# Layer 0's k and v from 15 block products each in place of 18, q plain; the third pair's table products within k's set; the feed-forward's last additions on GpSimd

## The chip, the cores and the metric

The kernel runs on one core of a Trainium2 chip. The metric is the device time of one execution in microseconds (us). A core has TensorE (PE; PEld is its loading of the stationary operand), VectorE (DVE), ScalarE (ACT), GpSimd (POOL) and SyncE (SP). ScalarE, VectorE and GpSimd work through queues in the order that is written for them; GpSimd and SyncE also issue most DMA transfers. Results of TensorE go to PSUM, eight banks of 128 x 512 numbers; everything else on the chip is in SBUF.

## What is computed

Two layers on eight images of 32 x 32 positions and 384 channels. Layer 0 is attention over all 1024 positions of an image, six heads of 64, with a table term that depends on the distance of rows and of columns; layer 1 is causal attention with one head of 384 and a feed-forward with binarized weights. Cut to what matters:

```python
qkv = x.reshape(b, hw, c) @ qkv_w + qkv_b           # x: group-normed image
attn = einsum('bqd,bkd->bqk', q * SCALE, k) + rel_h + rel_w
x = x + softmax(attn) @ v @ proj_w + proj_b         # layer 0
t = t + causal_attention(layer_norm(t))             # layer 1
h = gelu(quantize(layer_norm(t) @ sign(W1 - mean) + b1))
t = t + quantize(h @ sign(W2 - mean) + b2)
# quantize(y) = clip(y * 128 / (max|y| + eps), -128 + eps, 128 - eps); the feed-forward is zero for images 5 to 7
```

## The kernel before, in words

Images are taken in the order 5, 0, 1, 2, 3, 4, 6, 7 (`ORDER`). The feed-forward runs for 0 to 4; its ending for one image (`finish`, from the list `unfinished`) is issued within layer 0 of the next. Everything is float32, and the whole program is written out without loops on the chip. A scheduler orders each engine's queue as the program is built, by the order of the Python lines as far as data, buffers and explicit `issue_after` edges let it.

An image is held transposed, `xT` (`gnT`): channels on 128 partitions in three blocks, 1024 positions in the free dimension.

*Layer 0, products.* `project_qk` (L438) makes one third m of q or k: for each half of 512 positions three products of a 128 x 128 block of `wqkv_sb` (stationary) with 512 positions, added in one PSUM bank. m = 0 to 2 are q, 3 to 5 are k. `queries_keys` copies the two banks out, one on ScalarE (L468) and one on VectorE (L466); k is written with a stride of two. For images that follow a feed-forward, the products of m = 0 and 1 are made within it (`ahead`). `positions(p)` (L484) multiplies q of a pair p of heads with the table `rel`; ScalarE (L489) and VectorE (L490) copy the results out, and SP transfers turn them into `near` by way of DRAM (L496, L501). `values(j)` (L536) makes v for 128 positions: three products with positions as the stationary operand and 384 columns of weights. So k and v are 3 x 2 x 3 = 18 blocks of 128 x 128 by 512 each. `place(p)` rounds `near` to a high part (ScalarE, L517) and a remainder (VectorE, L519) and issues 16 transfers (L524), eight on SP and eight on POOL, into four image buffers `r`.

*Layer 0, attention.* For each pair and half, eight scores (L588, k with q, then L592, `r` with the fixed matrix `unit`), Exp on ScalarE (L598), sums on VectorE (L605), products with v (L613). Then the projection (L386).

*Layer 1* (L734, L386, L775, L790), during which the next image's group norm runs; then the feed-forward: first product L898, Gelu L924 and L925, second product L939, VectorE adds the bias (L940) and takes the maximum; GpSimd reduces it over partitions (L854), clips (L949), VectorE multiplies and adds to x (L953), and four output transfers are issued on POOL (L994).

*Buffers.* `image` is a pool of 11 buffers of 128 x 3080 numbers (images, q, k, v, r, x, weights of the feed-forward), `page` one of 12 buffers of 128 x 1024; every PSUM tile is one of the eight banks.

## Time and profile before

| what | us |
|---|---|
| median of 3 runs (2350.43 to 2351.89) | 2351.74 |
| the profiled execution, its own time | 2350.82 |
| its span, first to last instruction | 2348.8 |
| L438, 576 records, busy | 257.4 |
| L536, 384 records, busy | 125.2 |
| L484, 192 records, busy | 47.7 |
| L953, VectorE, 40 records, busy | 26.1 |
| L949, GpSimd, 40 records, busy | 30.5 |

A line of the profile's fifth part names the line of the kernel, engine and operation, result<-operands, shapes and count, then busy time and mean length of one, then the idle time of the engine just before and what ended it. Rows of time show start and length. Successive records of TensorE overlap, since the ends are modelled, so the distance of two starts tells what one costs. One float32 product stands as two load records and two matmul records.

### The profile page before, as it was taken

Reading aid. Unit: us, or ns where it says so; the run is one execution under the profiler, and the core shown is the slowest. Engines: PE = TensorE matmul, PEld = TensorE weight load, DVE = VectorE, ACT = ScalarE, POOL = GpSimd, SP = SyncE. Lnnn points to the kernel's source line nnn. Section 1 sums busy time; section 2 is a strip of 40 time slices with the busy share of each in tenths; the row PEclk is TensorE's granted clock in tenths of the full one; section 3 lists DMA queues with packets and bytes.
Section 4 is the critical chain, followed back from the end, with each engine's and each line's share of the span. In section 5 each row is a group of like instructions: output and inputs, shape, how many; then the busy total and the mean of one; then the engine's idle time right before and its main releaser. Section 6 shows DMA issues by size and latency. Waiting matters only on the chain.

```text
span 2348.8 us, 26174 instructions
## 1 busy us (share of the span) xinstructions
PE 2324.9 (99%) x9442; PEld 1288.2 (55%) x9442; DVE 1433.9 (61%) x2302; ACT 1041.7 (44%) x1763; POOL 316.6 (13%) x421
## 2 busy tenths in 40 slices
PE   7999999999999999999999999999999999999998
PEld 3445544568545577445684455864457744554454
DVE  3685568665587347684466864558734668525851
ACT  3551156137463256642365522747324656115621
POOL 0420013000230001310002300023000131001300
PEclk9999999999999999999999999999999999999999
DMA  6431361130631003520107211063101262017100
GB/s 166 146 117 37 104 146 38 54 135 1 144 99 68 20 21 91 118 88 14 41 12 166 65 68 41 1 138 105 68 1 41 68 139 63 1 51 146 45 1 29
DMA packets 154795, 169.99 MB, mean 72 GB/s; under 512 B 113408, under 2 KB 126048, under 8 KB 153120
## 3 DMA queue, kind: packets, MB, share of 16 engines
q1 hardware_dynamic: 134416, 98.93, 17.2%
q0 software_dynamic: 17184, 69.22, 9.7%
q8 instruction: 77, 1.26, 0.2%
q10 hardware_dynamic: 3056, 0.08, 0.1%
q14 instruction: 62, 0.51, 0.1%
HBM read 75.38 MB, written 42.47 MB: 50 GB/s over the span
## 4 chain that ended last, share of the span: by engine, by line
PE 99%; DVE 1%; DMA 0%; issue 0%; ACT 0%; DVEq 0%
PE f_s L588 14%; PE f_av L613 14%; PE f_qk L438 11%; PE f_s L775 8%; PE f_av L790 8%; PE f_y L939 7%; PE f_y L898 7%; PE f_pj L386 5%; PE f_v L386 5%; PE f_v L536 5%; PE f_q L734 5%; PE f_s L592 4%; PE f_rel L484 2%; PE f_pt L314 1%; PE f_den L631 0%; DMA f_gnT<-in_xT 0%
## 5 line engine op out<-in xcount | busy, mean ns | idle before, releaser
L598 ACT ACTIVATE f_pr<-f_s 128x512 f32<-128x512 f32 x768 | 413.6, 595 | 54.2 <-PE f_s L592 46.8
L588 PE MATMUL f_s<-f_q,f_k 64*128 64x512 f32 x1536 | 399.0, 595 | 0.0
L605 DVE TENSOR_TENSOR f_sum<-f_sum,f_pr 128x1024 f32<-128x1024 f32 x288 | 365.8, 1270 | 22.6 <-ACT f_pr L598 0.5
L613 PE MATMUL f_av<-f_pr,f_v 128*64 128x512 f32 x1536 | 339.4, 594 | 0.0
L592 PE MATMUL f_s<-f_r,unit 64*128 64x512 f32 x768 | 307.6, 792 | 0.0
L438 PE MATMUL f_qk<-f_gnT,wqkv_sb 128*128 128x512 f32 x576 | 257.4, 600 | 1.5 <-DVE f_gnT L349 1.5
L588 PEld LDWEIGHTS f_s<-f_q,f_k 64*128 64x128 f32 x1536 | 145.7, 186 | 127.4 <-issue 67.3
L613 PEld LDWEIGHTS f_av<-f_pr,f_v 128*64 128x64 f32 x1536 | 106.2, 137 | 196.3 <-issue 192.4
L775 PE MATMUL f_s<-f_q,f_lnT 128*128 128x512 f32 (+3 forms) x576 | 195.9, 488 | 0.0
L790 PE MATMUL f_av<-f_v,f_pr 128*128 128x385 f32 x576 | 195.3, 486 | 0.0
L438 PEld LDWEIGHTS f_qk<-f_gnT,wqkv_sb 128*128 128x128 f32 x576 | 108.0, 191 | 143.2 <-issue 131.5
L784 ACT ACTIVATE f_pr<-f_s 128x512 f32<-128x512 f32 (+3 forms) x96 | 47.1, 491 | 267.7 <-DVE f_s L780 220.7
L524 POOL DMA_DIRECT2D f_r<-f_far x192 | 102.2, 535 | 461.7 <-DVE f_far L519 450.9
L790 PEld LDWEIGHTS f_av<-f_v,f_pr 128*128 128x128 f32 x576 | 108.2, 190 | 77.3 <-issue 11.5
L775 PEld LDWEIGHTS f_s<-f_q,f_lnT 128*128 128x128 f32 x576 | 102.0, 190 | 77.8 <-issue 53.8
L902 ACT ACTIVATE f_h<-f_y,b_sb 128x256 f32<-128x256 f32 x240 | 100.9, 472 | 67.5 <-PE f_y L898 66.9
L909 DVE TENSOR_REDUCE am<-f_h 128x1 f32<-128x1024 f32 (+2 forms) x80 | 71.5, 946 | 96.3 <-ACT f_h L902 96.3
L734 PE MATMUL f_q<-f_lnT,wqk 128*128 128x512 f32 x288 | 127.5, 592 | 0.0
L386 PE MATMUL f_pj<-wproj_sb,f_oT 128*128 128x384 f32 x384 | 127.3, 488 | 0.0
L386 PE MATMUL f_v<-wv_sb,f_lnT 128*128 128x384 f32 x384 | 126.5, 486 | 0.0
L536 PE MATMUL f_v<-wqkv_sb,f_gnT 128*128 128x384 f32 x384 | 125.2, 486 | 0.0
L592 PEld LDWEIGHTS f_s<-f_r,unit 64*128 64x128 f32 x768 | 75.1, 187 | 90.0 <-issue 90.0
(153 smaller groups left out, 3024.9 us busy)
## 6 DMA issues: line engine op xcount, KB each, us to landing
f_far<-f_far SPq DMA_DIRECT2D x48, 512.0 KB, 3.2
f_r<-f_far POOLq DMA_DIRECT2D x192, 128.0 KB, 3.9
f_r<-f_far SPq DMA_DIRECT2D x192, 128.0 KB, 3.2
f_gnT<-in_xT SPq DMA_DIRECT2D x24, 512.0 KB, 4.6
f_x<-in_x SPq DMA_DIRECT2D x32, 384.0 KB, 7.5
out_y<-f_x POOLq DMA_DIRECT2D x28, 384.0 KB, 4.4
f_far<-f_far SPq DMA_DIRECT2D x128, 64.0 KB, 4.9
f_w1a<-w1s POOLq DMA_DIRECT2D x5, 1536.0 KB, 7.0
```

What stands on the lines that cost most here:

```text
L386: nc.tensor.matmul(ps[:, :C], xT[:, k, ts(j, P)], w[:, k, cols], start=(k == 0), stop=(k == NC - 1))
L438: nc.tensor.matmul(made[half], wqkv_sb[:, i, ts(m, P)], xT[:, i, ts(half, 512)], start=(i == 0), stop=(i == NC - 1))
L536: nc.tensor.matmul(ps, keys[:, i, j // 2, j % 2], wqkv_sb[:, i, 2 * C :], start=(i == 0), stop=(i == NC - 1))
L588: nc.tensor.matmul(sc[par], k[rows[par], p, ts(c, P)], q[rows[par], p, ts(half, 512)], start=True, stop=False)
L592: last_matmul[0] = nc.tensor.matmul(sc[par], unit[rows[par], c // 2 % 2].rearrange("i h w -> i (h w)"), r[2 * (c // 4) + c % 2][rows[par], ...
L598: last_exp[0] = nc.scalar.activation(pr[:, ts(par, 512)], sc[par], AF.Exp).ins
L605: adds.append(nc.vector.tensor_tensor(total, total, pr, ALU.add).ins)
L613: last_matmul[0] = nc.tensor.matmul(av[ts(par, HD), :], v[:, c, ts(2 * p + par, HD)], pr[:, ts(par, 512)], start=(c == 0), stop=(c == NJ - 1),
L734: nc.tensor.matmul(ps, wqk[:, k, ts(m, P)], xT[:, half, k, :], start=(k == 0), stop=(k == NC - 1))
L775: nc.tensor.matmul(sc[:, lo:], xT[:, c // 4, k, ts(c % 4, P)], q[:, half, k, lo:], start=(k == 0), stop=(k == NC - 1),)
L790: nc.tensor.matmul(av[:, : C + 1], prs[c][:, ts(j - c, P)], v[:, c, :], start=(c == 0), stop=(c == j))
L898: nc.tensor.matmul(ps, w1k[i // 2][:, ts(m, P)], xs[i % 2][:, half, i // 2, :], start=(i == 0), stop=(i == 2 * NC - 1))
```

## The change

k and v are each made by a scheme that multiplies a 3 x 3 block matrix (weights) with a 3 x 2 one (three channel blocks by two halves of positions) in 15 block products. Each product takes a sum of weight blocks (`weight_forms`, 15 forms for k and 15 for v, made once on GpSimd into `wf`) and a sum of image blocks (`image_forms`, ten made and five given; the same forms serve k and v; on VectorE for the first image, on GpSimd during layer 1 for the others). `ProductSet` runs the products in the order `PROD_ORDER` into six banks A to F. After ten of the products the running content of the bank is copied out on ScalarE (`keep`), while the bank goes on being added to; four pairs of such copies are subtracted on VectorE, and six final VectorE additions of a bank and a kept part write k or v. For v each product is four pieces with 128 positions as the stationary operand and 128 columns of weights. q stays as it was, from its own `wq_sb`.

All of these matmuls, q's and the tables' are chained in their written order (`in_turn`). The third pair's table products stand after k's fifth product; after the eighth and the eleventh, ScalarE's two rounding copies of the first pair's `near` are put between the bank copies; the load of the Exp table follows k's last bank copy. The first pair's remainders follow k's last addition.

In the feed-forward x is written to DRAM (`spilt`) and read back later, the activations lie in image buffers rather than pages, and the ending (scale and clip, second clip, addition to x) runs on GpSimd alone. The image pool has 10 buffers, the first pair's `near` lies in an image buffer, `r` takes three buffers rather than four. A second path for out-of-range sums, not taken with these inputs, stays plain.

```diff
...
+N_PROD = 15
+PROD_ORDER = (
+    ("A", 5, "m5"), ("B", 11, "m11"), ("C", 7, "m7"), ("A", 13, "n0"), ("B", 6, "n1"), ("D", 8, None),
+    ("A", 12, "n2"), ("B", 0, "n4"), ("E", 14, None), ("A", 4, "n3"), ("B", 1, "n5"), ("F", 9, None),
+    ("A", 10, "n6"), ("B", 3, None), ("A", 2, None),
+)
+PROD_ENDS = {
+    "D": ("n2", "n2", 0, 0, 1), "E": ("m7", "n3", 0, 1, 1), "F": ("n0", "n1", 1, 0, 1),
+    "B": ("m5", "m5", 1, 1, -1), "A": ("n4", "n4", 2, 0, -1), "C": ("n5", "n6", 2, 1, 1),
+}
+PROD_TILES = (0, 2, 1)
+PROD_COMBINE = {"n1": ("n0", "n1"), "n2": ("n2", "m11"), "n3": ("m7", "n3"), "n6": ("n5", "n6")}
+PROD_PAGES = (("m11", "n1"), ("m5", "n4"), ("n2", "m7"), ("n0", "n3"), ("n5", "n6"))
+X_MADE = (2, 5, 0, 1, 11, 4, 7, 13, 6, 12)
+X_GIVEN = {8: (0, 0), 14: (0, 1), 9: (1, 0), 3: (1, 1), 10: (2, 1)}
...
-        self.image_ = pool("image", 11)
+        self.image_ = pool("image", 10)
...
+    wf, wq_sb = tile_of("wf", [P, N_PROD, 2, P]), tile_of("wq_sb", [P, NC, C])
...
+        raw = [wq_sb]
         for i in range(3):
-            nc.sync.dma_start(out=wqkv_sb[:, :, ts(i, C)], in_=src[:, :, ts(i, C)])
+            if i:
+                raw.append(pools.flat(f"raw_{i}")[:, : NC * C].rearrange("p (k o) -> p k o", k=NC))
+            nc.sync.dma_start(out=raw[i], in_=src[:, :, ts(i, C)])
...
+        nc.scalar.mul(bqk_neg, bqk, -1.0)
...
+    def weight_forms(pools, eng, raw, s):
...
+        room = pools.page(f"wsum_{s}")
+        s1, s2 = room[:, :P], room[:, P : 2 * P]
...
+        def w(i, k):
+            return raw[:, k, ts(PROD_TILES[i], P)]
+        def f(r):
+            return wf[:, r, s - 1, :]
...
+        add(s1, w(0, 1), w(0, 2))
+        add(f(8), w(0, 0), s1)
+        add(s2, w(2, 0), w(2, 2))
+        add(f(9), w(2, 1), s2)
+        sub(f(14), w(0, 0), w(0, 1))
+        sub(f(14), f(14), w(1, 0))
+        add(f(5), w(0, 1), w(2, 0))
+        eng.tensor_scalar_mul(f(11), w(0, 1), -1.0)
+        eng.tensor_copy(f(13), w(2, 0))
+        add(f(6), f(5), w(2, 2))
+        add(f(12), s1, w(2, 0))
+        add(f(0), w(1, 1), s2)
+        add(f(4), s1, w(1, 0))
+        eng.tensor_copy(f(1), w(1, 1))
+        add(f(10), f(12), w(2, 2))
+        sub(f(10), f(10), w(1, 2))
+        slowest = last[0]
+        eng.tensor_copy(f(7), w(1, 0))
+        sub(f(3), w(2, 1), w(2, 0))
+        sub(f(3), f(3), w(1, 1))
+        add(f(2), w(1, 0), w(1, 1))
+        add(f(2), f(2), w(1, 2))
+        return slowest
...
+        def in_turn(*args, **kw):
+            with tc.issue_after(last_product[0]) if last_product[0] else contextlib.nullcontext():
+                last_product[0] = nc.tensor.matmul(*args, **kw).ins
...
+        def image_forms(b, xT, eng):
+            rooms = [pools.page(f"xf_{b}_{i}") for i in range(len(X_MADE) // 2)]
+            made = {r: rooms[i // 2][:, ts(i % 2, 512)] for i, r in enumerate(X_MADE)}
+            def x(k, n):
+                return xT[:, k, ts(n, 512)]
+            def add(r, a, b, op=ALU.add):
+                eng.tensor_tensor(made[r], a, b, op)
+            def sub(r, a, b):
+                add(r, a, b, ALU.subtract)
+            f = made
+            sub(5, x(2, 1), x(0, 1))
+            sub(5, f[5], x(1, 1))
+            add(2, x(2, 0), x(2, 1))
+            sub(0, f[2], x(1, 0))
+            sub(1, x(1, 1), f[0])
+            add(11, f[1], x(0, 1))
+            sub(4, x(0, 0), f[2])
+            add(7, f[4], x(0, 1))
+            add(13, f[7], x(1, 1))
+            sub(6, x(1, 0), x(2, 0))
+            sub(12, x(2, 0), x(0, 0))
+            return made | {r: x(*at) for r, at in X_GIVEN.items()}
...
+        class ProductSet:
+            def __init__(self, b, s, forms):
+                self.name, self.s, self.forms = f"{b}_{s}", s, forms
+                self.at, self.banks, self.part, self.final = 0, {}, {}, None
+                self.left = {bank: sum(bank == o[0] for o in PROD_ORDER) for bank in "ABCDEF"}
+                self.full, self.behind = [], None
+            def kept(self, name):
+                if name not in self.part:
+                    pair = next(pair for pair in PROD_PAGES if name in pair)
+                    room = pools.page(f"u_{self.name}_{pair[0]}")
+                    self.part.update({n: room[:, ts(i, 512)] for i, n in enumerate(pair)})
+                return self.part[name]
+            def multiply(self, ps, r, start):
+                x, w = self.forms[r], wf[:, r, self.s - 1, :]
+                if self.s == 1:
+                    in_turn(ps, w, x, start=start, stop=True, skip_group_check=True)
+                    return
+                keys = x.rearrange("p (g i n) -> p g n i", g=2, n=2)
+                for j in range(4):
+                    in_turn(
+                        ps[:, ts(j, P)], keys[:, j // 2, j % 2], w, start=start and j == 0, stop=True, skip_group_check=True
+                    )
+            def keep(self, ps, name):
+                dst = self.kept(name)
+                end = next((end for end in PROD_ENDS.values() if end[0] == name), None)
+                with tc.issue_after(self.behind) if self.behind else contextlib.nullcontext():
+                    if self.s == 2 or end is None:
+                        self.last_copy = nc.scalar.copy(dst, ps).ins
+                        return
+                    m = NPAIR + end[2]
+                    bias = (bqk if end[4] > 0 else bqk_neg)[:, m : m + 1]
+                    self.last_copy = nc.scalar.activation(dst, ps, AF.Identity, bias=bias).ins
+            def run(self, n, final=None):
+                self.final = final or self.final
+                for self.now in range(self.at, self.at + n):
+                    bank, r, name = PROD_ORDER[self.now]
+                    start = bank not in self.banks
+                    if start:
+                        self.banks[bank] = pools.o_tile(f"pr_{self.name}_{bank}")
+                    self.left[bank] -= 1
+                    self.multiply(self.banks[bank], r, start)
+                    if name is not None:
+                        self.keep(self.banks[bank], name)
+                    if name in PROD_COMBINE:
+                        dst, other = PROD_COMBINE[name]
+                        nc.vector.tensor_tensor(self.part[dst], self.part[dst], self.part[other], ALU.subtract)
+                    if not self.left[bank]:
+                        self.full.append(bank)
+                    self.finish()
+                self.at += n
+            def finish(self):
+                while self.final and self.full:
+                    bank = next((f for f in self.full if self.ready(f)), None)
+                    if bank is None:
+                        return
+                    self.full.remove(bank)
+                    name, _, p, half, sign = PROD_ENDS[bank]
+                    self.last_final = self.final(self.banks.pop(bank), self.part[name], p, half, ALU.add if sign > 0 else ALU.subtract)
+            def ready(self, bank):
+                return PROD_ENDS[bank][1] in [o[2] for o in PROD_ORDER[: self.now + 1]]
...
-                    nc.tensor.matmul(
-                        made[half], wqkv_sb[:, i, ts(m, P)], xT[:, i, ts(half, 512)], start=(i == 0), stop=(i == NC - 1)
+                    (in_turn if pools.fast else nc.tensor.matmul)(
+                        made[half], w[:, i, ts(m, P)], xT[:, i, ts(half, 512)], start=(i == 0), stop=(i == NC - 1)
...
-            r = []
+            rooms = {}
+            def r(part, p):
...
+                i, at = divmod(4 * (p % 2) + part, NPAIR)
+                if i not in rooms:
+                    rooms[i] = pools.flat(f"r_{b}_{i}", F32R)
+                return rooms[i][:, ts(at, T)]
...
-                    if half:
+                    if half and not (pools.fast and b == ORDER[0]):
...
+            def round_off(d, near, pages):
+                hi, _, src = both(near, pages, d)
+                return nc.scalar.copy(hi, src).ins
...
+                    hi, lo, src = both(near, pages, d)
+                    if not rounded:
+                        with behind_of(behind[0]):
+                            round_off(d, near, pages)
+                    with behind_of(behind[1]):
                         nc.vector.tensor_tensor(lo, src, hi.bitcast(F32), ALU.subtract)
...
+            def put_keys(ps, kept, p, half, op):
+                dst = k[:, p, ts(half, 512)].rearrange("d (g n i) -> d g i n", n=2, i=P)
+                ps, kept = (t.rearrange("d (g i n) -> d g i n", n=2, i=P) for t in (ps, kept))
+                return nc.vector.tensor_tensor(dst, ps, kept, op).ins
+            def put_values(ps, kept, p, half, op):
+                ps, kept = (t.rearrange("t (j c) -> t j c", j=4) for t in (ps, kept))
+                return nc.vector.tensor_tensor(v[:, 4 * half : 4 * half + 4, ts(p, P)], ps, kept, op).ins
...
+            def products():
+                forms = xf.pop(b)
+                of_k, of_v = (ProductSet(b, s, forms) for s in (1, 2))
+                for m in range(NPAIR):
+                    queries_keys(m)
+                    if m:
+                        near.append(positions(m - 1))
+                of_k.run(5, put_keys)
+                near.append(positions(NPAIR - 1))
+                if unfinished:
                     unfinished.pop()()
-                    early = pools.small.tile([P, 1], F32, tag="early", name=f"early0_{b}")
-                    nc.scalar.activation(early, k[:, 0, T - 1 :], AF.Exp, scale=0.0)
-            for j in range(NJ):
-                values(j)
-            r.extend(pools.image(f"r_{b}_{part}", F32R) for part in range(4))
-            place(0, *near[0])
+                for d in range(2):
+                    of_k.run(3)
+                    with behind_of(of_k.last_copy):
+                        of_k.behind = round_off(d, *near[0])
+                of_k.run(N_PROD - of_k.at)
+                place(0, *near[0], (None, of_k.last_final), rounded=True)
+                early = pools.small.tile([P, 1], F32, tag="early", name=f"early0_{b}")
+                with behind_of(of_k.last_copy):
+                    of_v.behind = nc.scalar.activation(early, of_k.part["n5"][:, 0:1], AF.Exp, scale=0.0).ins
+                of_v.run(N_PROD, put_values)
...
+                            r(2 * (c // 4) + c % 2, p)[rows[par], ts(half, 512)], start=False, stop=True,
...
+            spilt = store.tile([P, NJ * C], F32, tag="spilt", bufs=2, name=f"{pools.path}_spilt_{b}")
...
+                    last_product[0] = last_transpose[0]
+                    ahead[AFTER[b], 0] = project_qk(AFTER[b], gn, 0, plain[0])
...
+            nc.sync.dma_start(out=spilt, in_=xt.rearrange("p j c -> p (j c)"))
...
+            def activate(room, j, m0, m1):
...
+                hi, lo = (room[:, i, m0:m1, :] for i in range(2))
...
+                room = pools.flat(f"hilo_{b}_{j}", F32R)[:, : 3 * T].rearrange("p (i m q) -> p i m q", i=2, q=P)
...
+                if j == 4:
+                    xt = pools.flat(f"xagain_{b}")[:, : NJ * C].rearrange("p (j c) -> p j c", j=NJ)
+                    nc.sync.dma_start(out=xt.rearrange("p j c -> p (j c)"), in_=spilt)
...
-            s, ga = absmax_scale(am2, f"2_{b}")
-            up = pools.small.tile([P, 1], F32, tag="qu", name=f"qu_{b}")
-            nc.vector.tensor_scalar_mul(up, ga, (QB - QEPS) / QB)
-            low = pools.small.tile([P, 1], F32, tag="ql", name=f"ql_{b}")
-            nc.vector.tensor_scalar_mul(low, up, -1.0)
+            s, _ = absmax_scale(am2, f"2_{b}")
             for j in range(NJ):
-                nc.gpsimd.tensor_scalar(y[:, j, :], y[:, j, :], up, low, ALU.min, ALU.max)
+                nc.gpsimd.tensor_scalar(y[:, j, :], y[:, j, :], s, QB - QEPS, ALU.mult, ALU.min)
             def add():
                 for j in range(NJ):
-                    nc.vector.scalar_tensor_tensor(xt[:, j, :], y[:, j, :], s, xt[:, j, :], ALU.mult, ALU.add)
+                    nc.gpsimd.tensor_scalar_max(y[:, j, :], y[:, j, :], QEPS - QB)
+                    nc.gpsimd.tensor_tensor(xt[:, j, :], y[:, j, :], xt[:, j, :], ALU.add)
+                return xt
...
+                xf[ORDER[0]] = image_forms(ORDER[0], gn, nc.vector)
+                with tc.issue_after(weight_forms(pools, nc.gpsimd, raw[1], 1)):
+                    weight_forms(pools, nc.gpsimd, raw[2], 2)
...
-                        yield from group_norm_T(AFTER[b])
+                        norm = group_norm_T(AFTER[b])
+                        made = next(norm)
+                        yield made
+                        next(norm, None)
+                        if pools.fast:
+                            xf[AFTER[b]] = image_forms(AFTER[b], made, nc.gpsimd)
...
```

## The prediction

> **What bounds the kernel now.** I read the busy times first, then the chain of waits, then TensorE's rows in order of time around one image's layer 0.
>
> ```profile
> PE 2324.9 (99%) x9442; PEld 1288.2 (55%) x9442; DVE 1433.9 (61%) x2302; ACT 1041.7 (44%) x1763; POOL 316.6 (13%) x421
> PEclk9999999999999999999999999999999999999999
> ...
> PE 99%; DVE 1%; DMA 0%; issue 0%; ACT 0%; DVEq 0%
> ```
>
> TensorE works or is modelled busy for 99% of the span at the full granted clock, and 99% of the chain that ended last is TensorE's own. Between 14.3 us and the closing test of the sums no row of it waits for more than 0.3 us. So a TensorE row that goes away shortens the kernel by its own spacing, as long as nothing new makes TensorE wait; and a wait that appears costs its full length.
>
> The rows of time (start, length, engine) of the image that begins at 595 us, one with a feed-forward ahead of it:
>
> ```profile
> 604.47 5.42 PE L438 MATMUL f_qk<-f_gnT,wqkv_sb 128*128 128x512 f32 x12
> 609.82 1.99 PE L484 MATMUL f_rel<-f_q,rel 64*128 64x512 f32 x8
> 611.74 10.57 PE L438 MATMUL f_qk<-f_gnT,wqkv_sb 128*128 128x512 f32 x24
> 622.14 15.64 PE L536 MATMUL f_v<-wqkv_sb,f_gnT 128*128 128x384 f32 x48
> 637.71 1.13 PE L588 MATMUL f_s<-f_q,f_k 64*128 64x512 f32 x4
> ```
>
> Lengths overlap at their ends, so I take differences of starts. k, the third table product and v last from 604.47 to 637.71, 33.24 us. Each product stands as two records. k: 5.35 + 10.40 = 15.75 us for 18 products, 0.858 us each (10.30 us for 12 in the chain of waits) and 0.3 us for changes between shapes. Table product: 1.92. v: 15.57 us for 24, 0.645 each. Image by image this stretch repeats eight times.
>
> **k.** 15 products of the same shape as L438: 15 x 0.858 + 0.3 = 13.17 us, 2.58 less per image.
>
> **v.** 15 products of four pieces, each 128 columns wide, two records each: 120 records. The nearest row is the last diagonal block of layer 1's scores, six records of that shape (start, length):
>
> ```profile
> 255.13 0.83 PE L775 MATMUL f_s<-f_q,f_lnT 128*128 128x128 f32 x6
> 255.80 2.44 PE L790 MATMUL f_av<-f_v,f_pr 128*128 128x385 f32 x7
> ```
>
> 0.67 us for six is 0.112 us a record, so 120 x 0.112 = 13.44 us. From below: if records went at the rate per column of L438 (0.429 us for 512 columns), 0.107, 12.87 us. From above: the stationary operand here is every second token, as in L536, whose load records take 196 ns where L775's take 190; if all 6 ns came on top, 0.118, 14.16 us. I take 0.115, 13.8 us: 1.77 less per image.
>
> The Trainium skill speaks against this part: "TensorE: Matmul & The Clock Gate", section "LDWEIGHTS (loading the stationary operand)", has a load cost its number of columns over 1.2 ns, so 107 ns however few columns follow it. By that estimate loads alone are 120 x 0.107 = 12.8 us, and the row, at 112 ns, agrees that a piece this narrow is no faster than its load.
>
> **What ScalarE now puts in TensorE's way.** A bank is copied out in the middle of its accumulation, and its next product must wait for that copy. I run the k set with t = 0 at its first product. Durations: a product 0.858; copy with bias 0.68 (L468, q), plain 0.59 (L660); from a product's end to ScalarE's start 0.31 (597.21 + 3 x 0.858 = 599.78, ScalarE starts at 600.09); back to TensorE 0.15 (L333 ends 10.74, TensorE starts 10.89). Now two rounding copies stand between the bank copies, by order:
>
> ```profile
> 616.85 1.07 ACT L517 CAST f_far<-f_near 64x1024 fp32r<-64x1024 f32 x1
> 624.78 1.99 ACT L517 CAST f_far<-f_near 64x1024 fp32r<-64x1024 f32 x1
> ```
>
> Five products to 4.29, the third table product to 6.21, D8, A12, B0 to 8.79. n4 is copied 9.10 to 9.78, first rounding to 10.85, n3 10.85 to 11.53, n5 (B1 ends 11.37) 11.68 to 12.36, second rounding to 14.35, n6 to 14.96. A10 ended at 13.08 and B3 at 13.94; A2, which adds into the bank that n6 is read from, starts at 15.11. That is a wait of 1.17 us in each image, and everything of TensorE's chained order is behind it. The earlier copies are done at least 0.4 us before they are needed: m5 is ready for A13 at 2.16 (ScalarE has the second table product's copies until 1.3), needed at 2.57. In the v set no rounding stands there; n6 is ready 0.31 + 0.59 + 0.15 = 1.05 after A10 while B3 covers 0.9: 0.15 us. The Exp table load (1.28) now falls between the sets, ahead of a copy needed only 1.8 us after its product.
>
> Stretch per image: 13.17 + 1.92 + 1.17 + 13.80 + 0.15 = 30.21 in place of 33.24: 3.03 saved, **24.2 us** for eight.
>
> **VectorE.** Per set four combinations (678 ns, VectorE's row of L657) and six final additions: k's write with the stride of L466 (1.12), v's near L666 (0.69). The k set, copies of the table product (2.8) and the rounding remainders (1.2 and 1.95) run to about t = 22 in my order, the v set's additions end about 1.8 after the last product; v is first read by L613, 8.9 us later. The banks: six of eight per set, the last three of k freed by t = 19, when v has three. Nothing on the path; without that cover a late k addition would delay the first scores one for one.
>
> **GpSimd.** The feed-forward's ending moves there on five images. VectorE loses 8 x 0.70 (L953), which were hidden. The rows of time (in brackets the idle time before and what ended it):
>
> ```profile
> 604.09 6.10 POOL L949 TENSOR_SCALAR f_y<-f_y,qu,ql 128x384 f32<-128x384 f32 x8 [6.90 <-PE f_rel L484]
> ...
> 665.74 8.53 POOL L567 TENSOR_TENSOR f_x<-f_x,pb 128x384 f32<-128x384 f32 x8 [8.13 <-DMA f_x<-in_x]
> ...
> 673.33 2.02 DVE L603 TENSOR_TENSOR f_sum<-f_pr,f_pr 128x1024 f32<-128x1024 f32 x1 [2.83 <-ACT f_pr L598]
> ```
>
> Undisturbed, a clip takes 0.65 and an addition 1.0. From 604.1 (t = -0.4): eight first passes to 4.8, eight times clip and addition, 13.2, to 18.0; four output issues at 0.75, to 21. But the two engines hold each other up: L603 took 2.02 in place of 1.23 while L567 ran, and L949 once 1.33 while L953 ran. VectorE's two-input work here is four combinations (2.7) and the remainders; I add 4 us: 25. Behind, on the same queue, are the eight issues of the first pair's table (L524, 0.53 each, 3.9 to landing), which the first scores wait for (L592). Part 0 lands at 25 + 0.5 + 3.9 = 29.4, v ends at 30.2 and L592 follows 0.56 later. Parts 2 and 3 are read 4.4 us on. Just in time; I put 0.5 us on each of five images, 2.5. From below: nothing, and from above: 1.0 more on each addition, as L567's slowest (2.07), 33 in place of 25, a wait of 6.6 or so. The SP half of the table needs only the rounding, t = 14.4, and is early.
>
> The Trainium skill has this as an exclusive lock ("SBUF — State Buffer", section "SBUF: two separate sides"): a GpSimd instruction and a VectorE one with two SBUF inputs never share the port pair, the later blocks. By it GpSimd loses at most VectorE's two-input time, 2.7 + 3.15 = 5.9 us, and ends at 27.
>
> **The rest.** The next image's eleven forms run on GpSimd (1.26 each, its own row of L657 where nothing disturbs it, some 14 us) beside layer 1's scores, where its only other work is issues that now wait until about 817 us of this execution and are needed at 838. In the first image VectorE makes them (11 x 0.68) from 15.7 while GpSimd makes 21 weight forms (0.4 each, a third of L567's 1.0 or L181's half-height 0.40) from about 14: with each excluding the other both are done by 33, and k begins at 35.6. VectorE's table copies may come late there: 0 to 2, I take 1. Spilling x and reading it back are two more SP transfers of 1.5 MB, which land in about 7 us (the median of w1a); the write is over before the last feed-forward buffer is needed, 16 us later, the read has four blocks of 4.2 us. Activations in two image buffers: ScalarE may pause about 1 us at the third block, where it is over 2 ahead. Nothing. If that cover is gone, each wait costs its length five times.
>
> **Sum.** Span 2348.8 - 24.2 + 2.5 + 1 = 2328. Around the span lie 2.0 us (the profiled execution took 2350.8), so 2330, and the median of the runs shown is 0.9 above it: **2331**.
>
> **Rivals.** *ScalarE is not in the way* (18%): the second rounding starts earlier or latencies are shorter, and v goes at 0.112. Then the stretch is 13.17 + 1.92 + 13.44 = 28.53, 4.71 saved, 37.7 in all: 2314. For it: no row shows a mid-bank copy waited for. Against: the order puts 1.99 us right ahead of n6.
>
> *The table arrives late* (15%, slower): GpSimd ends so late that L592 waits on five images. The gain of 23.2 is gone at 4.6 us a piece. With all eight additions at 2.07 and the output issues still ahead, GpSimd ends at 33, part 0 lands at 37.4, 6.6 after it is due: 33 us, 10 more than the gain, 2361. For it: the two-second-long rows of L567 and L603. Against: those stood beside L605's unbroken additions, and VectorE here has under 6 us of such work.
>
> *The copies eat it all* (9%): three more waits like the 1.17 in each image, since every bank of these sets is read while it is filled, or a buffer held too long now that there are ten image buffers: 3 x 8 = 24 us, 2352, no change. Against: 0.4 us of slack at each.
>
> **How the numbers follow.** The forecast has 58%, alone 2321 to 2341 (v at 0.107 or 0.118, GpSimd's wait 0 to 2 us). Faster by over 0.2% (4.7 us, about what a measurement tells from no change) is the forecast, the first rival and a little of the third: 78%. Within it 7%, slower 15%. The range goes from the first rival to just short of no change, 2313 to 2350.
>
> **What would show it.** k as 240 records 0.429 apart and v as 960 records 0.11 to 0.12 apart; an idle time of TensorE near 1.2 us ahead of the fifteenth k product, ended by ScalarE; none over 0.3 in the v set; L592's loads not waiting for a table transfer by more than 1 us. Wrong it would be if v's records stood at 0.13 or more (1.8 us a piece, 14 in all), if TensorE idled before L592 on five images, or in L898 and L939, where I expect nothing.

## The result, and the profile after

The changed kernel takes **2417.0 us** (median of 4 runs, 2416.1 to 2423.5), the kernel before 2351.8 beside it: a ratio of 1.0283, 95% interval 1.0264 to 1.0302. It is 65 us slower where 21 us less were forecast. The profiled execution has a span of 2414.4 us, 65.6 more than before.

From the page after, the busy times, the clock and the chain that ended last:

```profile
PE 2327.5 (96%) x9970; PEld 1347.2 (56%) x9970; DVE 1518.0 (63%) x2364; ACT 1090.6 (45%) x1874; POOL 566.8 (23%) x620
...
PEclk9999999999899999899998999998999989999999
...
PE 89%; POOL 7%; DMA 2%; DVE 1%; ACT 1%; issue 1%; SPq 0%; POOLq 0%; ACTq 0%
```

TensorE's share falls from 99% to 96%. GpSimd, which did not appear in the chain before, holds 7% of it now, with DMA 2% behind it, and the granted clock is below nine tenths in five slices: five, like the images with a feed-forward ahead of them.

What TensorE waited for (us in total, times, the longest):

```profile
PE f_s L808 <- DMA f_r<-f_far: 42.3, 5, 9.1
...
PE f_s L804 <- ACT f_pr L814: 8.5, 16, 0.7
PE f_pr_A L505 <- ACT f_u_n L566: 7.0, 8, 0.9
PE f_y L1158 <- DVE f_hilo L1141: 5.3, 5, 1.1
```

None of the four stood in the kernel before. L804 and L808 are the scores (L588 and L592 before), L1158 the second product of the feed-forward (L939).

TensorE's rows of time for the image that the prediction followed (start, length):

```profile
606.45 1.99 PE L505 MATMUL f_rel<-f_q,rel 64*128 64x512 f32 x8
608.37 1.12 PE L505 MATMUL f_pr_A<-f_xf,wf 128*128 128x512 f32 x2
...
621.74 1.02 PE L505 MATMUL f_pr_B<-f_gnT,wf 128*128 128x512 f32 x2
623.64 1.13 PE L505 MATMUL f_pr_A<-f_xf,wf 128*128 128x512 f32 x2 [0.87 <-ACT f_u_n L566]
624.60 1.10 PE L505 MATMUL f_pr_A<-wf,f_xf 128*128 128x128 f32 x8
...
637.86 1.11 PE L505 MATMUL f_pr_A<-wf,f_xf 128*128 128x128 f32 x8
638.89 1.13 PE L804 MATMUL f_s<-f_q,f_k 64*128 64x512 f32 x4
648.44 0.80 PE L808 MATMUL f_s<-f_r,unit 64*128 64x512 f32 x2 [8.41 <-DMA f_r<-f_far]
```

From the first k product to the first score it is 638.89 - 608.37 = 30.52 us, 33.24 before. The gain is there. Then the first reader of the table stands still for 8.41 us.

GpSimd's rows over the same time:

```profile
608.03 12.39 POOL L1164 TENSOR_SCALAR f_y<-f_y,qs 128x384 f32<-128x384 f32 x8 [6.95 <-PE f_rel L505]
620.40 2.31 POOL L1168 TENSOR_SCALAR f_y<-f_y 128x384 f32<-128x384 f32 x2
622.69 1.95 POOL L1169 TENSOR_TENSOR f_xagain<-f_y,f_xagain 128x384 f32<-128x384 f32 x2
...
631.37 3.37 POOL L1169 TENSOR_TENSOR f_xagain<-f_y,f_xagain 128x384 f32<-128x384 f32 x2
...
639.77 3.09 POOL L1224 DMA_DIRECT2D out_y<-f_xagain  x4
642.86 3.71 POOL L708 DMA_DIRECT2D f_r<-f_far  x7
```

Eight first passes of 1.55 us, eight maxima and additions (19.4 us together), four outputs, and only then, at 642.86, the first issue of the table; the first score was ready for it at 639.5.

By stage, against the kernel before, as differences of starts:

| stage | change, us |
|---|---|
| k, third table product and v, eight images | -22.1 |
| first eight scores to second eight scores (15.9 before, but in the first image): five images behind a feed-forward, 29.8 to 31.3 | +72.4 |
| the same in the other three: 18.7 and 20.2, and 25.2 in the first image (21.9 before) | +10.3 |
| second product of the feed-forward, five images | +5.2 |
| the rest | -0.2 |
| span | +65.6 |

So the loss is in one place, the first eight scores of each image: 82.7 us.

### The profile page after: what moved, and what is told of

Its sections match the earlier page's. It is cut to its first block, busy times and chain, and to the rows that moved or that the text cites. A ratio compares the mean times of both kernels' runs of the same rounds, so it can differ in the third digit from the quotient of the medians.

```text
span 2414.4 us, 27759 instructions
## 1 busy us (share of the span) xinstructions
PE 2327.5 (96%) x9970; PEld 1347.2 (56%) x9970; DVE 1518.0 (63%) x2364; ACT 1090.6 (45%) x1874; POOL 566.8 (23%) x620
## 3 DMA queue, kind: packets, MB, share of 16 engines
q1 hardware_dynamic: 135856, 114.66, 20.2%
## 4 chain that ended last, share of the span: by engine, by line
PE 89%; POOL 7%; DMA 2%; DVE 1%; ACT 1%; issue 1%; SPq 0%; POOLq 0%; ACTq 0%
PE f_s L804 14%; PE f_av L829 14%; PE f_s L991 8%; PE f_av L1006 8%; PE f_y L1116 7%; PE f_y L1158 7%; PE f_qk L505 5%; PE f_pj L455 5%; PE f_v L455 5%; PE f_q L950 5%; PE f_s L808 4%; POOL f_y L1164 2%; POOL f_y L1168 2%; POOL f_xagain L1169 2%; PE f_pt L383 1%; PE f_rel L505 1%
## 5 line engine op out<-in xcount | busy, mean ns | idle before, releaser
L804 PE MATMUL f_s<-f_q,f_k 64*128 64x512 f32 x1536 | 426.5, 617 | 8.5 <-ACT f_pr L814 8.5
L808 PE MATMUL f_s<-f_r,unit 64*128 64x512 f32 x768 | 334.6, 813 | 42.3 <-DMA f_r<-f_far 42.3
L804 PEld LDWEIGHTS f_s<-f_q,f_k 64*128 64x128 f32 x1536 | 165.3, 192 | 138.8 <-issue 62.3
L808 PEld LDWEIGHTS f_s<-f_r,unit 64*128 64x128 f32 x768 | 90.1, 194 | 128.6 <-issue 80.1
L516 POOL TENSOR_TENSOR f_xf<-f_gnT 128x512 f32<-128x512 f32 x28 | 35.5, 1279 | 502.6 <-DVE f_gnT L418 502.6
L819 DVE TENSOR_TENSOR f_sum<-f_pr,f_pr 128x1024 f32<-128x1024 f32 x48 | 61.0, 1270 | 130.8 <-ACT f_pr L814 130.8
L1158 PE MATMUL f_y<-f_w2a,f_hilo 128*128 128x384 f32 x640 | 128.5, 341 | 5.3 <-DVE f_hilo L1141 5.3
L505 PE MATMUL f_qk<-f_gnT,wq_sb 128*128 128x512 f32 x288 | 129.5, 601 | 1.7 <-DVE f_gnT L418 1.7
```

Source lines behind the costliest of these rows:

```text
L505: last_product[0] = nc.tensor.matmul(*args, **kw).ins
L804: nc.tensor.matmul(sc[par], k[rows[par], p, ts(c, P)], q[rows[par], p, ts(half, 512)], start=True, stop=False)
L808: last_matmul[0] = nc.tensor.matmul(sc[par], unit[rows[par], c // 2 % 2].rearrange("i h w -> i (h w)"), r(2 * (c // 4) + c % 2, p)[rows[pa ...
L1158: nc.tensor.matmul(ps[:, :C], h, w, start=(i == 0), stop=(i == len(products) - 1))
```

## The experiments

All times are medians, and each has the kernel before beside it on the same chip (2351.8 to 2353.0, so a difference of 1 us between experiments on different chips says nothing); ratios are to it, and differ from the quotients of these medians by up to 0.0006. "To the values" means from an image's first score to the first product with v: 8.9 us before; in the changed kernel 22.8 to 24.3 us behind a feed-forward and 11.6 and 13.2 in two others. The first image stands apart, 14.9 before and 18.2 changed, since TensorE also makes `f_wqk` in that stretch. In the diffs "..." stands for lines left out.

**The ending put back** (e1_end_back).

```diff
...
-                nc.gpsimd.tensor_scalar(y[:, j, :], y[:, j, :], s, QB - QEPS, ALU.mult, ALU.min)
+                nc.gpsimd.tensor_scalar(y[:, j, :], y[:, j, :], up, low, ALU.min, ALU.max)
...
-                    nc.gpsimd.tensor_scalar_max(y[:, j, :], y[:, j, :], QEPS - QB)
-                    nc.gpsimd.tensor_tensor(xt[:, j, :], y[:, j, :], xt[:, j, :], ALU.add)
+                    nc.vector.scalar_tensor_tensor(xt[:, j, :], y[:, j, :], s, xt[:, j, :], ALU.mult, ALU.add)
```

> The changed kernel with the feed-forward's ending put back: one clip a block on GpSimd (min and max with two pointers), VectorE multiplies by s and adds. Theory A (on five images GpSimd issues the first pair's table transfers late because its ending lasts until t = 31): the first eight scores of these five images fall from 30 us to about 20, the length that they have in images without a feed-forward, TensorE's wait at the table's first reader goes to under 1 us there, and the time to about 2417 - 5 x 10.5 = 2365 us. Rival B (only the order of SP's queue is at fault): no change, 2417. Rival C (GpSimd's lateness is the whole loss): 16 us for the first eight scores, 2345.

2362.4 us, 1.0047 (1.0030 to 1.0063): 55 us less than the changed kernel. The wait for the table is gone, and the five images take 11.6 to 12.1 us to the values, as the others do. Theory A holds and rival B falls; rival C falls too, for all images still miss 2.7 us (the first 3.2). VectorE, which adds again, now makes TensorE wait 2.2 us, in five times (L505, for the copies of a table product).

**The same GpSimd instructions, later in the queue** (e2_end_later).

```diff
...
-                if unfinished:
-                    unfinished.pop()()
...
-                place(0, *near[0], (None, of_k.last_final), rounded=True)
+                placed = place(0, *near[0], (None, of_k.last_final), rounded=True)
+                if unfinished:
+                    with tc.issue_after(placed):
+                        unfinished.pop()()
```

> The changed kernel with the same GpSimd instructions, but the maxima, additions and output issues placed behind the first pair's table issues on GpSimd's queue; the first passes stay ahead. Theory A (the place in the queue is what costs, not contention with VectorE): table issues done at t = 25 or so, first eight scores 20 us on the five images, time about 2365. Additions then end at about t = 45 and the second pair's table, read at t = 63, is in time. Rival D (GpSimd's work slows VectorE's remainders or ScalarE, wherever it stands): first eight scores stay above 25, time above 2390.

2360.0 us, 1.0032 (1.0018 to 1.0047). No instruction was taken away, and the 57 us are back: the place in the queue was the cost, not the work. Rival D falls.

**Another form of the same ending** (e3_clip_scale): clip by two pointers, then multiply, then add.

```diff
...
-                nc.gpsimd.tensor_scalar(y[:, j, :], y[:, j, :], s, QB - QEPS, ALU.mult, ALU.min)
+                nc.gpsimd.tensor_scalar(y[:, j, :], y[:, j, :], up, low, ALU.min, ALU.max)
...
-                    nc.gpsimd.tensor_scalar_max(y[:, j, :], y[:, j, :], QEPS - QB)
+                    nc.gpsimd.tensor_scalar_mul(y[:, j, :], y[:, j, :], s)
```

> The changed kernel with the same number of GpSimd passes, but the first is min and max with two pointers (0.65 us in the kernel before) and the second multiplies by s. Theory A: the 1.55 us belong to that form with a multiplication and an immediate; if the clip takes 0.65 and the multiplication alone about as much as the maximum (1.3), GpSimd ends 7 us earlier and each of five images gains 5 to 7: 2382 to 2392. If the multiplication takes 1.55 instead, 5 us earlier, 2392 to 2397. Rival E (every one-input pass takes 1.3 to 1.55 here since VectorE holds GpSimd up): no change, 2417.

2370.2 us, 1.0074 (1.0057 to 1.0091), 47 less than the changed kernel, so more than expected. GpSimd's groups (after the bar: busy us, mean ns of one), first of the changed kernel, then of this one:

```profile
L1164 POOL TENSOR_SCALAR f_y<-f_y,qs 128x384 f32<-128x384 f32 x40 | 62.0, 1561 | 34.8 <-PE f_rel L505 27.6 <-ACT f_far L666 7.1
L1168 POOL TENSOR_SCALAR f_y<-f_y 128x384 f32<-128x384 f32 x40 | 50.9, 1286 | 0.0
L1169 POOL TENSOR_TENSOR f_xagain<-f_y,f_xagain 128x384 f32<-128x384 f32 x40 | 48.0, 1217 | 0.0
```

```profile
L1172 POOL TENSOR_SCALAR f_y<-f_y,qs 128x384 f32<-128x384 f32 x40 | 49.3, 1242 | 0.0
L1173 POOL TENSOR_TENSOR f_xagain<-f_y,f_xagain 128x384 f32<-128x384 f32 x40 | 39.1, 997 | 0.0
L1168 POOL TENSOR_SCALAR f_y<-f_y,qu,ql 128x384 f32<-128x384 f32 x40 | 25.6, 647 | 35.9 <-PE f_rel L505 21.5 <-ACT f_far L666 14.3
```

On one shape a clip with two pointers takes 0.65 us, a multiplication by a pointer 1.24, a maximum with a constant 1.14 undisturbed (1.29 in the mean), a multiplication with a minimum 1.56. The prediction had priced every pass like the clip. Rival E falls, since the clip takes 0.65 us in the very place where the multiplication with a minimum took 1.56. Ending some 9 us sooner (outputs done 25.6 us after the first pass began, 609.29 to 634.92, in place of 34.8) is nearly enough for the table: two short waits are left, 2.5 us in all. A new one, 3.9 us in five, stands at a bank copy (L505, for `f_u_m`).

**SP's order** (e4_sp_order). The third pair's transfers are issued behind the first pair's table; `bring` holds the transfers that `positions` issued.

```diff
...
-                near.append(positions(NPAIR - 1))
+                near.append(positions(NPAIR - 1, False))
...
                 place(0, *near[0], (None, of_k.last_final), rounded=True)
+                bring(NPAIR - 1, [page.bitcast(F32) for page in near[-1][1]], near[-1][0])
```

> The changed kernel with the third pair's table transfers (writes to DRAM and reads back) issued on SP behind the first pair's table instead of ahead of most of it; products and copies unmoved. Theory F (in the images without a feed-forward SP's half of the table is held up behind the third pair's reads): their first eight scores fall from 18.7 to 20.2 us to about 16, 10 us in three images, and the other five images stay as they are, since GpSimd's half is later still: 2407. Rival G (the slow scores there come from something else, the clock or the copies of the scores): no change, 2417.

2417.0 us, 1.0277 (1.0258 to 1.0296): no change. Theory F falls; in the images without a feed-forward little came of it (11.2 to the values, 11.65 in the last image of the changed kernel).

What is it then that costs every image 2.7 us? The rows of the last image of the kernel with the ending put back show it:

```profile
2153.21 0.68 DVE L732 TENSOR_TENSOR f_v<-f_pr_D,f_u_n 128x512 f32<-128x512 f32 x1
2153.76 1.13 PE L804 MATMUL f_s<-f_q,f_k 64*128 64x512 f32 x4
...
2155.20 1.08 ACT L814 ACTIVATE f_pr<-f_s 128x512 f32<-128x512 f32 x2 [2.64 <-PE f_s L808]
...
2155.85 1.18 PE L804 MATMUL f_s<-f_q,f_k 64*128 64x512 f32 x3 [0.73 <-ACT f_pr L814]
2156.20 0.68 DVE L732 TENSOR_TENSOR f_v<-f_pr_A,f_u_m 128x512 f32<-128x512 f32 x1
```

The second scores start 2.1 us after the first (1.2 before) and wait for the Exp of the first ones, though VectorE had emptied v's bank D two microseconds earlier. Two theories: the six additions of v, all behind its last combination, hold six of the eight banks; or the second and third scores were simply given the first scores' banks when the program was laid out.

**v's additions earlier** (e5_v_first), in the kernel of the second experiment: three of them ahead of the last combination.

```diff
...
-                        nc.vector.tensor_tensor(self.part[dst], self.part[dst], self.part[other], ALU.subtract)
+                        with behind_of(self.last_final if self.s == 2 and name == "n6" else None):
+                            nc.vector.tensor_tensor(self.part[dst], self.part[dst], self.part[other], ALU.subtract)
```

> The kernel of e2_end_later, with VectorE's order in the v set changed: three of the six final additions (banks D, E, F) stand ahead of the last combination, and are done 2 to 5 us before v's last product. What is left in every image is that the second and third of the first scores wait 0.5 to 0.7 us each for ScalarE's exponentials, and the first eight scores take 11.65 us to the start of the values in place of 8.92. Theory H (the second and third scores were given, when the program was laid out, the banks of the first scores, so that they wait for the exponentials whatever VectorE does): no change, 2360. Rival I (it is the six additions that hold the banks too long): 2.7 us per image, 2338.

2360.9 us, 1.0036 (1.0023 to 1.0050): no change. In the last image the three additions end 1.5 us ahead of the first score (2149.98 and 2151.48), and the next scores still wait for ScalarE (9.6 us, 16 times in the eight images; 9.7 without the edit). Emptying the banks sooner brings nothing, and rival I falls.

**Other banks, same order** (e5b_banks). On the kernel of the second experiment, an edge without a semaphore, from the first Exp of an image to v's last addition, tells the scheduler that v's banks come free first.

```diff
...
                     last_exp[0] = nc.scalar.activation(pr[:, ts(par, 512)], sc[par], AF.Exp).ins
+                    if p == c == half == 0 and values_end:
+                        tc.add_manual_dep(
+                            last_exp[0], values_end[-1].name,
+                            mybir.DependencyInfo(mybir.DependencyClass.NoSync, mybir.DependencyReason.DATA), reason="order",
+                        )
```

> The kernel of e2_end_later, with the same instructions in the same order on every engine, but the banks of the second and third scores are those that v's additions free (D, E, F, C) and not those of the first scores. Theory H: the additions free them 0.1, 0.7, 1.3 and 1.9 us after the last product and the scores need two every 1.09 us, so nearly all of the 2.7 us per image goes: 2338 to 2344. Rival I (VectorE's late additions): no change, 2360, since the additions come no earlier.

**2340.9 us**, 0.9949 (0.9934 to 0.9965): 19 us less, and faster than the kernel before. ScalarE, VectorE and GpSimd run the same instructions in the same order as without the edge. To the values it takes 8.9 us in images without a feed-forward, as before (15.8 in the first), and 9.5 to 10.2 behind one. Of its waits:

```profile
PE f_pr_A L505 <- ACT f_u_n L566: 6.8, 8, 0.9
PE f_y L1166 <- DVE f_hilo L1149: 5.2, 5, 1.1
...
PE f_s L807 <- DVE f_v L733: 0.3, 1, 0.3
```

The scores no longer wait for ScalarE. Theory H holds.

**The changed kernel with these banks alone** (f4_after_banks): the same edge, and the ending where the change put it.

> The changed kernel with nothing but the banks of e5b_banks (the second and third of an image's first scores in the banks that v's additions free); GpSimd's ending stays ahead of the table's issues. Theory H with A (the two losses add up): 2.7 us in each of eight images, 2417 - 22 = 2395, and the first eight scores of the five images with a feed-forward still take 10 us more than in the others. Rival O (the late table covers the banks on the five images): 2.7 us in three images alone, 2409.

2392.1 us, 1.0165 (1.0150 to 1.0181): 25 us less than the changed kernel, so the two losses add up, and a little more. Rival O falls.

**The kernel before with the ending alone on GpSimd** (e8_before_end): the change's own three lines in `ffn`, nothing else.

> The kernel before with one part of the change alone: the feed-forward's ending on GpSimd (multiplication and minimum, maximum, addition). Theory A: GpSimd needs 8 x 1.55 + 8 x 2.5 = 32 us from 604.1 of the profile before, outputs 3.1, so part 0 of the table lands at about 645, 7 us after the first scores need it, and the scores after a stop of that length go at half the rate for some us: 10 to 12 us on each of five images, 2402 to 2412. Rival J (the ending is only in the way since k and v are shorter): under 3 us on each of five images, 2352 to 2367.

2391.8 us, 1.0172 (1.0156 to 1.0188). The direction and mechanism are A's; the price is 39 us, not 50 to 60. Its waits for the table are 26.8 us, 5.4 each in place of 7: k and v last 2.7 us longer there and give GpSimd that much more time. Rival J falls: the ending costs without the shorter k and v too.

**Everything at once** (e7_all): the banks, the additions earlier, the second rounding copy whole behind the copy of n6, and ScalarE's activations cut by cut. The last two edits:

```diff
...
-                for d in range(2):
-                    of_k.run(3)
+                for n in (3, N_PROD - 8):
+                    of_k.run(n)
                     with behind_of(of_k.last_copy):
-                        of_k.behind = round_off(d, *near[0])
+                        of_k.behind = round_off(int(n > 3), *near[0])
...
-                nc.scalar.activation(hi, part, AF.Gelu, scale=s)
-                nc.scalar.activation(part, part, AF.Gelu, scale=s)
+                with tc.issue_after(cut_[0]) if cut_[0] else contextlib.nullcontext():
+                    nc.scalar.activation(hi, part, AF.Gelu, scale=s)
+                cut_[0] = nc.scalar.activation(part, part, AF.Gelu, scale=s).ins
```

> The kernel of e2_end_later with the banks of e5b_banks, the additions of e5_v_first, the second rounding copy placed behind the copy of n6 (theory: the wait ahead of the fifteenth k product, 0.9 to 1.1 us in eight images, is the rounding copy ahead of n6 on ScalarE), and ScalarE's activations of a feed-forward block kept in the order high and full of one cut, then of the next (theory: the wait of 1.06 us in the second block on five images comes from both high parts going ahead of the full ones). If all three hold: 2360 - 22 - 7 - 5 = 2326 us. If the wait before the fifteenth product has another cause, 2333; if that in the feed-forward has, 2331.

2353.9 us, 1.0004 (0.9995 to 1.0013), 13 us worse than the banks alone. Three edits, three misses, and the first eight scores alone are 13 us longer. The wait ahead of the fifteenth k product became one in the v set (L505 waits for f_u_m, 5.9 us in eight). The feed-forward's wait stayed 5.3. And v's reordered VectorE work ran into GpSimd's additions, which now stand there (VectorE, GpSimd and a score that waits, one image):

```profile
949.63 3.51 DVE L589 TENSOR_TENSOR f_u_n<-f_u_n 128x512 f32<-128x512 f32 x1
950.64 1.94 POOL L1180 TENSOR_TENSOR f_xagain<-f_y,f_xagain 128x384 f32<-128x384 f32 x2
...
953.06 0.68 DVE L734 TENSOR_TENSOR f_v<-f_pr_B,f_u_m 128x512 f32<-128x512 f32 x1
...
953.89 0.85 PE L807 MATMUL f_s<-f_q,f_k 64*128 64x512 f32 x1 [1.92 <-DVE f_v L734]
```

A combination of 0.69 us lasts 3.51, the additions for banks B, C and A stand behind it, and the scores wait for them: 7.6 us in four images.

**The rounding copy in two halves** (f1_round_split), one ahead of n6, one behind, on the kernel with the banks.

```diff
...
-                for d in range(2):
-                    of_k.run(3)
+                for n, d, part in ((3, 0, slice(0, H)), (3, 1, slice(0, H // 2)), (N_PROD - 11, 1, slice(H // 2, H))):
+                    of_k.run(n)
                     with behind_of(of_k.last_copy):
-                        of_k.behind = round_off(d, *near[0])
+                        of_k.behind = round_off(d, *near[0], part)
```

> The kernel of e5b_banks with the second rounding copy (2.0 us on ScalarE) cut into two halves of 1.0, one ahead of the copy of n6 and one behind it. Theory K (the wait of 0.85 to 0.9 us ahead of the fifteenth k product is that rounding copy; placed whole behind n6 in e7_all it only moved the wait to the v set's first copy): ScalarE has a gap of about 1.0 us ahead of n6 and one of 2 behind it, so both halves fit and eight waits go: 2341 - 7 = 2334. Rival L (the latency from product to copy and back to product is the wait, whatever stands ahead of n6): no change, 2341.

2339.6 us, 0.9949 (0.9934 to 0.9965). All eight waits are gone and k and v are 0.9 us shorter in each image, so K names the cause rightly and rival L falls. But the ratio is that of the banks alone: of 7 us nothing arrives that the measurement could tell. The table is late instead in three images, and in three the second eight scores lose 1.5 us each, where they wait for ScalarE (L806).

```profile
PE f_s L810 <- DMA f_r<-f_far: 3.2, 3, 1.4
...
PE f_s L806 <- ACT f_oT L883: 1.2, 3, 0.4
```

**VectorE's order in the feed-forward** (f2_low_first). On the kernel with the banks, the second block's first low part goes ahead of the first block's bias addition; the two Gelus that it needs move up with it.

```diff
...
-                nc.vector.tensor_tensor(y[:, j, :], ps[:, :C], b2_sb, ALU.add)
+                if j == 0:
+                    room = pools.flat(f"hilo_{b}_1", F32R)[:, : 3 * T].rearrange("p (i m q) -> p i m q", i=2, q=P)
+                    early_low = activate(room, 1, 0, 6)
+                with tc.issue_after(lows[0]) if j == 0 else contextlib.nullcontext():
+                    nc.vector.tensor_tensor(y[:, j, :], ps[:, :C], b2_sb, ALU.add)
```

> The kernel of e5b_banks with VectorE's order in the second linear layer changed at one place: the low part of the second block's first cut stands ahead of the first block's addition of the bias. Theory M (the wait of 1.06 us in the second block, on five images, is that low part queued behind an addition that itself waits for the first block's last product): the wait goes, 2341 - 5 = 2336. Rival N (ScalarE's activations are what is late, through the two image buffers): no change, 2341.

2337.7 us, 0.9936 (0.9921 to 0.9952): 3.2 us less, some 1 us of which is the chip, and the intervals overlap. The trace is clearer: the wait falls from 5.2 to 2.0 (L1171, five times 0.4). Since ScalarE's order moved too, this run alone does not part M from N. In the changed kernel's rows the Gelu that the low part needs ends at 897.73, and the low part starts only at 898.72, behind the bias addition and the maximum (897.65 to 898.80); and in the run with everything at once ScalarE's order was put back and the wait stayed. So M holds for the larger part.

**Both** (f3_best).

> The kernel of e5b_banks with both the split rounding copy of f1_round_split and the order of f2_low_first. If theories K and M hold and add up: 2341 - 7 - 5 = 2329 us, 1.0% under the kernel before. If only one holds: 2334 or 2336.

2337.1 us, 0.9936 (0.9922 to 0.9949). They do not add up, as far as differences this small can tell; waits of the scores for the table are 4.1 us in four. It is 15 us, 0.6%, faster than the kernel before and 80 us faster than the changed one, with the change's arithmetic untouched. Earlier table issues in this kernel were not tried.

## Why the prediction was wrong

Two of the signs that the prediction had named as wrong came: TensorE idles before the table's reader on five images, and in the feed-forward's second product.

**k and v were right.** k's records stand as forecast. v's piece cost the upper bound: 624.60 to 637.86 is 14 products of eight records, 118 ns a record where 115 was taken. The copy of n6 behind the second rounding copy made TensorE wait, as worked out: A2 starts 1.04 us late (623.64 in place of 621.74 + 0.86), 1.17 forecast, and the split copy removes it. The stretch is 30.5 us, forecast 30.2. No wait stands in the v set.

**The step that failed first is GpSimd's sum**: "eight first passes to 4.8, eight times clip and addition, 13.2, to 18.0". In the same time scale (0 at the first k product) the first passes ended at 12.0, maxima and additions at 31.4, outputs at 34.5 where 25 was written. The error is a price, not the order of work: a multiplication with a minimum was priced like L949's minimum and maximum, 0.65, and took 1.55; a maximum with a constant took 1.14 to 1.4. First passes 8 x 0.9 = 7.2 us and maxima 8 x 0.6 = 5 us too cheap; the 4 us put in for contention covered the additions' 1.7. Bounding L1164 from L567 (1.0, two inputs) or from twice L949 would have shown that the table was not just in time. The rival "the table arrives late" had the right wait at 15%, with 6.6 us a piece (8.5 in the mean came), but for another reason: it put all additions at 2.07 us, and they took 1.22.

**The second is a wait that nobody priced**: "The banks: six of eight per set ... Nothing on the path". The sum followed when k's banks come free and when v's additions end, which did not matter. What mattered is which banks the next tiles had been given. Scores 2 and 3 got those of score 1, and wait for ScalarE: 19 us by the experiment on the banks.

**The third is the feed-forward**, where "Nothing" was written: 5.2 us. The cover that was named, ScalarE two microseconds ahead, was not the one that counted. VectorE's low part stood behind an addition that waits for the block before: in the kernel before it started at 880.85, ahead of that addition (881.73); in the changed kernel at 898.72, behind it (897.65).

**The price of a late table** was also too low in kind. The rule was "a wait that appears costs its full length"; it costs more, for a stop of 8.4 us is followed by scores at half the clock. In the changed kernel (stretches of time; busy, granted clock, share of the DMA engines, GB/s):

```profile
639.00:648.00 9.00, 1.02 (x4) 0.68 0.81 258
648.00:652.00 4.00, 2.91 (x8) 0.50 0.40 128
652.00:656.00 4.00, 3.65 (x10) 0.50 0.00 0
656.00:660.00 4.00, 4.00 (x17) 0.60 0.00 0
660.00:664.00 4.00, 4.00 (x22) 1.00 0.00 0
```

The clock is 0.50 from the restart at 648.4 to about 659. The Trainium skill, "TensorE: Matmul & The Clock Gate", section 'Part 1: The HAM clock gate (the "warmup" mystery)', says that an idle window of some 3.4 us halves the clock and that a window as long of sustained work gives it back. The stops agree with the first half: after each of the 15 stops in the changed kernel, in the same with the other banks and in the kernel before with the ending on GpSimd, 4.7 to 10.0 us long, the clock is 0.50. But it also falls without such a window. In the changed kernel's image whose first score stands at 320.1, no table is late; two waits for a bank, 0.73 and 0.49 us, fall into one stretch of 3.41 us, and the next such stretch runs at half the clock:

```profile
321.32:324.73 3.41, 2.19 (x9) 1.00 0.06 24
324.73:328.14 3.41, 3.41 (x11) 0.50 0.00 0
```

This image takes 13.2 us to the values in place of 11.65. Two images of the second experiment's kernel show the same (13.1 and 13.3), none of the first experiment's, with the same waits. Here the measurement decides.

For the second half, the holes count: after the stop the bank waits leave TensorE 2.91 and 3.65 busy of 4.00, and the half clock lasts 10.8 us from the restart, in the other four images 8.3 to 8.7. With the other banks the scores run without holes, and it lasts 3.8 to 5.9 us, here 5.3 (restart at 645.0):

```profile
648.00:650.00 2.00, 2.00 (x8) 0.50 0.00 0
650.00:652.00 2.00, 2.00 (x14) 0.91 0.00 0
```

So the edge on the banks, the only difference of the two kernels, also shortens the half clock, in the five images from 44.9 to 23.5 us after the restart, though the stops are a little longer (8.3 to 10.0 us against 8.0 to 9.1). This goes with the 25 us that the banks brought in the changed kernel, against 19 where the table was in time.

The 82.7 us are then 42.3 us of waiting for the table, about 19 to 21 for the banks in all eight images, and some 20 left for the half clock (82.7 less the other two; an estimate, since waits and slow records overlap), the least certain of the three.

**Other points.** The first image gained 2.7 us in its stretch (35.2 before, not 33.24), 2.8 in the others, where 1 us less was put in. "The SP half of the table ... is early" was never the limit: moving it changed nothing.

## What to carry to other kernels

Price an operation that moves to another engine by the same operation there, or by the dearest of its neighbours: on GpSimd two passes of one shape and one input differed by 2.4 times. Then look at what is queued behind it: the ending was harmless work in a harmful place, and moving it behind eight transfer issues was worth 57 us with no instruction removed. When a set of banks is held longer, ask which banks the next tiles have been given, not when the old ones come free. And price a wait of TensorE by its length and the half clock behind it: here a stop of 4.7 to 5.6 us (the kernel before with the ending on GpSimd) cost 7 to 9 us.

## What the runs showed of the hardware

- **GpSimd's one-input passes** on 128 x 384 float32: minimum and maximum with two pointers 0.65 us, multiplication by a pointer 1.24, maximum with a constant 1.14 undisturbed, multiplication and minimum 1.56. An addition of two tensors took 0.98, less than three of the four.
- **VectorE beside GpSimd.** A VectorE subtraction of two 128 x 512 tensors in SBUF took 0.69 us in the median alone. In the kernel of the second experiment it took 0.75 to 0.82 beside a GpSimd maximum alone, 0.69 to 1.14 beside multiplications with a minimum alone, and 1.5 to 2.2 where a GpSimd addition ran as well (in the changed kernel 0.68 to 1.01, 0.69 to 1.11 and 0.7 to 1.5); in the kernel with everything at once 3.45 to 3.54, where a pair of additions began behind its start. The Trainium skill, "SBUF — State Buffer", section "SBUF: two separate sides", has such a VectorE instruction and a GpSimd one that reads SBUF exclude each other over a shared port pair for a whole instruction. The longest rows beside additions agree in kind; beside a one-input pass the first two kernels show 0.45 us or less, where the exclusion of a whole pass would cost up to 1.14 or 1.56.
- **The half clock lasts as long as the work has holes**: 8.3 to 10.8 us after a stop in five images where the restart was patchy, 3.8 to 5.9 in five where it was dense. From its fall to its end it lasted 3.41, 6.8, 10.2, 13.7 or 17.1 us, whole multiples of 3.41, and the shortest of these came after two waits of 0.73 and 0.49 us, without a stop.
